# Two fused layers on one core: layer 1's experts computed on pairs sorted by expert

## The chip, the core and the metric

The program runs on one core of a Trainium2 chip. Five engines work side by side: TensorE (PE in the profile, its weight loads PEld), VectorE (DVE), ScalarE (ACT), GpSimd (POOL) and SyncE (SP), which issues most transfers. The metric is the device time in microseconds (us). The kernel before took 1327.2 us as the median of three runs (1326.11 to 1327.76).

## The reference

Four rows of 512 tokens with 128 channels pass through two layers. Both layers add an attention and a mixture of experts to the row, each computed from the same layer-normed input. Everything is float32.

- Layer 0, attention: for 16 heads and a band of 64 earlier positions, differences of projections pass through two 16 by 16 products with an exact GELU. The result is a logit for each of the 64 positions. A softmax over the band weighs the values.
- Layer 0, experts: 16 experts with a gated activation, the best four of a token weighted by a softmax.
- Layer 1, attention: 16 heads of 8 channels over all 512 positions of the row.
- Layer 1, experts, which the change is about:

```python
score = relu(xf @ rw1 + rb1) @ rw2 + rb2
_, topi = top_k(score, 2)
mask = zeros(bool).at[arange(T)[:, None], topi].set(True)
gate = softmax(where(mask, score, -inf))
for e in range(8):
    h = relu(xf @ W1[e] + b1[e])        # 128 -> 512
    y = h @ W2[e] + b2[e]               # 512 -> 128
    out = out + gate[:, e:e + 1] * y
```

The gate of an expert that a token did not choose is zero, so only two of the eight experts of a token reach its output.

## The kernel before

The state `x1` stays in SBUF: 16 tiles of 128 tokens by 128 channels, four to a row. Work is written as Python generators that yield at chosen points. `woven` takes a list of generators, each with the number of its yields, and always advances the one that is least far along. That sets the order in which instructions are written down. A planner then orders the instructions of each engine by that order, by priority (`tc.high_priority` moves some ahead) and by its own cost estimates; on each engine the final order is fixed.

**Layer 0** goes row by row. `band_logits(b)` (L555 to L637) runs 64 steps. Each subtracts shifted projections on DVE (L572, about 2000 elements a partition), applies the GELU on ACT (L574, L578), and reduces over channels on PE with four column tiles side by side (L586, high priority). `gated_experts(b)` (L659) holds the 16 experts of layer 0: products at L688, L695 and L675, DVE work at L671 to L673. `prepare(b+1)` projects the next row. Each row is woven in two parts: the first 24 steps of the logits (30 in row 0), then the other 37.

`band_values(b-1)` finishes the attention of the row before: skewed copies through DRAM (L314 to L344), products at L353 and L357. It stands in the first part of the next row.

`relu_experts(b)` is layer 1's mixture of experts. It normalises the row into `xn` and transposes it into `xT` (L408), which layer 1's attention also reads. It computes the router (L388 with `rw1`, L418), ranks the scores and makes a row of gates for each expert. Those rows go to DRAM and come back spread over all partitions (L444). For each of the 8 experts and each of four chunks of 128 hidden channels, `hidden` multiplies 128 weight columns by all 512 tokens of the row (L388) and applies the relu on ACT (L396). Four products for the expert before sum the second layer (L454). DVE multiplies by the gate row (L458) and POOL adds to `total` (L459). In float32 one matmul is recorded as two passes on PE. So a row has 8 x 8 matmuls of 512 columns, all experts for all tokens.

The experts of row b-1 are woven half into the second part of row b and half into the first part of row b+1. Row 2's second half and all of row 3's experts fall into layer 1.

**Layer 1's attention**, `full_attention`, is a list of steps. A step has two products of scores (L970, four row tiles side by side): one set is reduced to its maximum on DVE (L987), the other is exponentiated on ACT (L994). Every second step weighs values (L883). All of these have high priority. Explicit dependencies keep them in order; the next set of products waits for the reduction and the exponential that free its PSUM bank. `pace` holds the list of these products. Each `hidden` product is made to come after the product that was last in `pace` when it was written, which spreads the experts over the steps.

SP issues nearly all transfers in order: route rows, expert weights, the band's copies, stores of `out`. POOL issues only the zero fill at the start. `out` of a row is stored right after its attention is added (L918), for the last row at the very end (L1006).

Of the kernel before, what the change touches and what calls it, by code (L numbers as in the profile page):

```python
# [22 lines left out]
FP = mybir.dt.float32  # L23
AF = mybir.ActivationFunctionType
ALU = mybir.AluOpType
# [3 lines left out]
P = 128  # L29
# [10 lines left out]
F1 = 512  # L40
LIMIT = 7.0
# [5 lines left out]
    "ident": 128, "hmask": 8, "mask8": 8, "lt16": 256, "lt8": 64, "ones8": 1, "rep": 128,  # L47
}
# [10 lines left out]
def shape_constants():  # L59
# [13 lines left out]
        "rep": (p[:, None] == m[None, :] % BD),  # L73
    }
# [23 lines left out]
def two_layers(ctx: ExitStack, tc: tile.TileContext, w: dict, consts: bass.AP, out: bass.AP):  # L98
# [47 lines left out]
    rows = keep.tile([37, 128], FP, name="rows")  # L146
    nc.sync.dma_start(out=rows[0:32, :], in_=w["L1_ffn_b1"].rearrange("e (c f) -> (e c) f", f=128))
    nc.sync.dma_start(out=rows[32:36, :], in_=w["L1_ffn_rb1"].rearrange("(c f) -> c f", f=128))
    nc.sync.dma_start(out=rows[36:37, :], in_=w["L0_ffn_scale"][None, :])
# [18 lines left out]
    b2_1 = keep.tile([E1, C], FP, name="b2_1")  # L168
    nc.sync.dma_start(out=b2_1, in_=w["L1_ffn_b2"])
# [68 lines left out]
    def routes(pool, tag, g, n, k, less, dst):  # L238
# [15 lines left out]
        nc.vector.tensor_scalar(rank, rank, float(k), None, ALU.is_lt)  # L254
# [41 lines left out]
    route_d = [[dram.tile([n, T], FP, name=f"route{n}_{b}") for b in range(B)] for n in (E0, E1)]  # L296
# [88 lines left out]
    def hidden(wt, bias, b, c):  # L385

        ph = bank()
        mm = nc.tensor.matmul(ph, wt[:, c * P:(c + 1) * P], xT[:, b * T:(b + 1) * T], start=True, stop=True)  # L388
        if pace:
            tc.add_manual_dep(  # L390
                mm.ins, pace[-1].ins.name,
                mybir.DependencyInfo(mybir.DependencyClass.NoSync, mybir.DependencyReason.DATA),
                reason="experts spread over the steps",
            )
        h = chain.tile([P, T], FP, tag="h", name="h", bufs=5)
        nc.scalar.activation(h, ph, AF.Relu, bias=bias[:, c:c + 1])  # L396
        return h

    def relu_experts(b):


        xn = chain.tile([P, TPB, C], FP, tag="o", name="xn", bufs=1)
        rw1 = chain.tile([C, F1], FP, tag="ew1", name="rw1")
        nc.sync.dma_start(out=rw1, in_=w["L1_ffn_rw1"])
        layernorm(b, xn)
        yield
# [4 lines left out]
        for c in range(4):  # L411
            hs.append(hidden(rw1, cols[:, 32:36], b, c))
# [14 lines left out]
        route = small.tile([P, TPB, E1], FP, tag="route1", name="route1")  # L427
        routes(small, "pairs", scores, E1, K1, c_("lt8"), route)
        yield
        rT = route_rows(small, route, E1, route_d[1][b], 1.0)  # L430
        py = bank()
        nc.tensor.matmul(py, b2_1, rT, start=True, stop=True)
        total = chain.tile([C, T], FP, tag="total", name="total", bufs=1)
        nc.scalar.copy(total, py)
        yield
        old = None
        for e in range(E1 + 1):
            if e < E1:
                w1 = chain.tile([C, F1], FP, tag="ew1", name="ew1")
                nc.sync.dma_start(out=w1, in_=w["L1_ffn_W1"][e])  # L440
                w2 = chain.tile([P, 4, C], FP, tag="ew2", name="ew2")
                nc.sync.dma_start(out=w2, in_=w["L1_ffn_W2"][e].rearrange("(c p) d -> p c d", p=P))
                r = chain.tile([P, T], FP, tag="r", name="r")
                nc.sync.dma_start(out=r, in_=route_d[1][b][e].partition_broadcast(P))  # L444
            new = []
            if old:
                py = bank()
            for c in range(4):
                if e < E1:
                    new.append(hidden(w1, cols[:, e * 4:e * 4 + 4], b, c))  # L450
# [590 lines left out]
```

## Time and profile before

| | |
|---|---|
| median of three runs | 1327.2 us |
| the profiled execution's own time | 1327.88 us |
| its span, first to last instruction | 1326.1 us |
| mean granted TensorE clock | 0.933 |
| row 0 of layer 0 | 36 to 235.8 us |
| row 1 | 235.8 to 463.3 us |
| row 2 | 463.3 to 696.2 us |
| row 3 | 696.2 to 909.5 us |
| layer 1 | 909.5 to 1326.1 us |

A line of a group gives the source line, the engine, the operation, the tiles written and read, the shapes and how many there were. After the first bar come the busy time in us and the mean of one in ns. After the second comes the time for which the engine was idle just before, with what ended it. A line of the table of stretches gives the stretch, its length, and for each engine the busy time with the number of instructions in brackets; then the granted clock as a share of full speed, the share of the 16 DMA engines that was busy, and GB/s. A line of a timeline gives the start and the length in us, then the instruction, with the idle time before it and what ended it in square brackets. A line of the waits gives the sum in us, how often, and the longest.

### The profile page before, as it was taken

The page shows a single profiled execution, that of the slowest core. Times are in us where ns is not written, and L with a number is a line of the kernel's source. Part 1 is how long each engine was busy: PE and PEld are TensorE (multiplying, and loading weights), DVE is VectorE, ACT ScalarE, POOL GpSimd, SP SyncE. Part 2 cuts the span into 40 slices and gives each one's busy share as a digit, 9 for nine tenths or more (in the row PEclk, how much of TensorE's full clock was granted, in tenths as well). Part 3 has the DMA queues.
Part 4 walks back from the last instruction along what each step waited for, and adds up shares of the span by engine and source line. Part 5 has one row for each costly group of instructions (what it writes and reads, how often), then busy time and mean ns, then how long its engine had stood idle before and what let it go on. Part 6 is the DMA issues. An engine that isn't in the chain of part 4 may idle for free. (4 is left out here: it accounts for less than half of the span.)

```text
span 1326.1 us, 17391 instructions
## 1 busy us (share of the span) xinstructions
PE 1140.2 (86%) x6727; PEld 438.3 (33%) x6727; DVE 1011.4 (76%) x1085; ACT 1004.9 (76%) x1142; POOL 76.5 (6%) x72
## 2 busy tenths in 40 slices
PE   4677887577879968998997899897999899999997
PEld 2122233132434423343341234433333334333332
DVE  4999998999977899998789999873655556445451
ACT  4899997989988899999879999994255445545554
POOL 2000000000000100100000010003100000000000
PEclk9798888778979989998999999998899999999999
DMA  8121111264412345551234555124453130120100
GB/s 279 42 86 54 61 60 55 101 155 113 125 52 61 96 136 141 134 156 49 72 100 140 139 143 148 56 79 145 110 112 95 48 73 15 40 66 24 49 24 9
DMA packets 170348, 120.75 MB, mean 91 GB/s; under 512 B 66909, under 2 KB 149562, under 8 KB 168730
## 3 DMA queue, kind: packets, MB, share of 16 engines
q1 hardware_dynamic: 168794, 112.91, 31.1%
q0 software_dynamic: 1184, 6.29, 1.2%
q8 instruction: 54, 0.88, 0.3%
q10 hardware_dynamic: 288, 0.43, 0.1%
q14 instruction: 28, 0.23, 0.1%
HBM read 90.57 MB, written 29.03 MB: 90 GB/s over the span
## 5 line engine op out<-in xcount | busy, mean ns | idle before, releaser
L572 DVE TENSOR_TENSOR z<-proj 128x2044 f32<-128x2044 f32 (+31 forms) x256 | 556.3, 2194 | 23.1 <-PE lbank L586 14.3
L586 PE MATMUL lbank<-z,place 128*32 128x504 f32 (+18 forms) x2048 | 291.3, 646 | 98.8 <-ACT z L578 54.7
L987 DVE TENSOR_REDUCE nmax<-score 128x2 f32<-128x1024 f32 x128 | 156.3, 1225 | 174.0 <-PE score L970 166.3
L578 ACT ACTIVATE z<-z,posb 128x1024 f32<-128x1024 f32 (+31 forms) x256 | 266.5, 1097 | 9.3 <-DVE z L572 7.4
L574 ACT ACTIVATE z<-z,brep 128x2048 f32<-128x2048 f32 (+31 forms) x128 | 240.7, 1907 | 7.8 <-DVE z L572 7.5
L994 ACT ACTIVATE ex<-score 128x1024 f32<-128x1024 f32 x128 | 130.5, 1024 | 145.2 <-PE score L970 145.2
L388 PE MATMUL bank<-xT,ew 128*128 128x512 f32 x256 | 140.1, 636 | 3.8 <-DVE e L628 3.8
L586 PEld LDWEIGHTS lbank<-z,place 128*32 128x32 f32 x2048 | 44.3, 114 | 272.2 <-ACT z L578 133.3
L454 PE MATMUL bank<-h,ew 128*128 128x512 f32 x256 | 131.2, 611 | 2.1 <-ACT h L396 2.1
L396 ACT ACTIVATE h<-bank,cols 128x512 f32<-128x512 f32 x144 | 98.1, 684 | 37.8 <-PE bank L388 36.7
L459 POOL TENSOR_TENSOR total<-total,part 128x512 f32<-128x512 f32 x32 | 55.0, 1719 | 1020.1 <-DVE part L458 820.1
L970 PE MATMUL score<-kpad,qpad 32*128 32x512 f32 x384 | 109.9, 645 | 4.1 <-DVE nmax L987 3.2
L970 PE MATMUL score<-qa,kpad 32*128 32x512 f32 x384 | 103.5, 648 | 2.2 <-ACT ex L994 2.2
L675 PE MATMUL accbank<-wT,lin 128*128 128x128 f32 x512 | 81.3, 295 | 17.1 <-DVE lin L673 17.1
L675 PEld LDWEIGHTS accbank<-wT,lin 128*128 128x128 f32 x512 | 71.3, 203 | 64.4 <-issue 31.8
L688 PE MATMUL gbank<-tT,wT 128*128 128x512 f32 x128 | 72.6, 651 | 11.3 <-DMA wT<-wT_all 7.4
L883 PE MATMUL accbank<-ex,vaug 128*32 128x512 f32 x512 | 70.4, 616 | 0.2 <-ACT ex L994 0.2
L695 PE MATMUL gbank<-tT,wT 128*128 128x512 f32 x128 | 69.3, 624 | 0.0
L454 PEld LDWEIGHTS bank<-h,ew 128*128 128x128 f32 x256 | 43.3, 190 | 62.6 <-issue 51.9
L388 PEld LDWEIGHTS bank<-xT,ew 128*128 128x128 f32 x256 | 41.2, 194 | 64.0 <-issue 48.8
L691 ACT ACTIVATE glu<-gbank,gbt 128x512 f32<-128x512 f32 x64 | 43.8, 685 | 14.6 <-PE gbank L688 13.8
L671 DVE SCALAR_TENSOR_TENSOR lin<-lin,r 128x512 f32<-128x512 f32 x64 | 47.2, 737 | 6.4 <-ACT lin L697 4.9
(198 smaller groups left out, 1226.2 us busy)
## 6 DMA issues: line engine op xcount, KB each, us to landing
r<-route SPq DMA_DIRECT2D x96, 256.0 KB
ew<-in_L_ffn_W SPq DMA_DIRECT2D x64, 256.0 KB
wb<-by_s SPq DMA_DIRECT2D x32, 512.0 KB
wT<-wT_all SPq DMA_DIRECT2D x48, 192.0 KB
by_t<-e SPq DMA_DIRECT2D x8, 1024.0 KB
f<-by_t SPq DMA_DIRECT2D x128, 64.0 KB
by_s<-g SPq DMA_DIRECT2D x16, 512.0 KB
wb<-by_s SPq DMA_DIRECT2D x24, 256.0 KB
```

The lines of the kernel that those rows point to most:

```text
L388: mm = nc.tensor.matmul(ph, wt[:, c * P:(c + 1) * P], xT[:, b * T:(b + 1) * T], start=True, stop=True)
L396: nc.scalar.activation(h, ph, AF.Relu, bias=bias[:, c:c + 1])
L454: nc.tensor.matmul(py, old[1][:, c, :], old[0][c], start=(c == 0), stop=(c == 3))
L572: nc.vector.tensor_tensor(z[:, :, :, 0:n], seen, own, ALU.subtract)
L574: nc.scalar.activation(z[:, :, :, 0:n], z[:, :, :, 0:n], AF.Gelu, bias=b_dmg)
L578: last = nc.scalar.activation(z[:, dq, :, 0:n], z[:, dq, :, 0:n], AF.Gelu, bias=posb[:, j:j + 1])
L586: mm = nc.tensor.matmul(ps[q:q + 32, t0:T], place[:, kind, 3 - dd:35 - dd], z[:, dq, hg, 0:n], start=(dd == 0), stop=(dd == 3),)
L675: nc.tensor.matmul(ya[:, i * P:(i + 1) * P], lin[:, i * P:(i + 1) * P], wT[:, 2, :], start=False, stop=(e == E0 - 1 and i == TPB - 1),)
L688: nc.tensor.matmul(pg, wT[:, 0, :], tT, start=True, stop=True)
L970: mm = nc.tensor.matmul(ps[:, h - two, :], own[r, i * P:(i + 1) * P], seen[r, :], start=True, stop=True)
L987: freed.append(nc.vector.tensor_reduce(nmax[n % 2][:, i, two:two + 2, 8:9], ps, AX.X, ALU.max, negate=True))
L994: freed.append(nc.scalar.activation(ex[n, i][:, two:two + 2, :], ps, AF.Exp, scale=inv))
```

## The change

The experts of layer 1 are computed for two rows at a time, and only for the pairs of a token and an expert that it chose. Two rows have 1024 tokens and 2048 pairs. Sorted by expert, each expert's list padded to a multiple of 128, they fill at most 23 blocks of 128 pairs. All 23 are computed, whatever the routing.

- `begin(b)` is the first part of `relu_experts`: norm, transpose, router and ranks. It also stores `xn` to DRAM (`xs_d`). The gate rows in DRAM and their broadcast are gone.
- `pairs(s)` handles rows 2s and 2s+1. Two products with a triangle and with ones count the tokens ahead of each token for each expert. Some DVE operations turn these into each pair's place in the sorted list. Sixteen products with selections built on DVE (`sel`) turn the places into the list of tokens of each block (`whose`) and a list of weight rows of each block (`which`).
- For each block POOL issues an indirect transfer of the block's expert weights and biases (128 rows of 1156 numbers, `wx`) and one of its 128 token rows (`xb`). PE transposes the rows, makes four products of 128 columns for the hidden layer, and four for the second layer one block later. The relus are split between ACT and DVE, the second bias is added on DVE, and SP stores the block (`ys_d`).
- At the end 16 indirect transfers fetch each token's two results, and 16 DVE operations add them to `x1` with their gates.
- Rows 0 and 1 are done in layer 0: `begin(0)` in the second part of row 1, `begin(1)` and 14 steps of `pairs(0)` in the second part of row 2, 24 steps of it in the first part of row 3, the rest and `begin(2)` in the second part of row 3. Rows 2 and 3 are done in layer 1 beside the attention, after the band values of row 3 and `begin(3)`.
- `wx` has two buffers in layer 0 and three in layer 1. `dense` in the attention has one buffer instead of two. `out` of rows 2 and 3 is stored at the end.
- The program receives an array `pair_weights` made from the weights by copying alone, and some more constants.

```diff
+NS = 2 * TPB
+NB = (NS * P * K1 + E1 * (P - 1)) // P
+WX = 2 * F1 + 4 + C
...
+    def begin(b, pool, deep):
...
+        nc.sync.dma_start(
+            out=xs_d[b // 2][b % 2 * T:(b % 2 + 1) * T, :].rearrange("(t p) c -> p t c", p=P), in_=xn
+        )
...
+    def pairs(s, pool, deep):
...
+        nc.tensor.matmul(pt[:, 0:NS * E1], c_("upper"), flat, start=True, stop=True)
+        nc.tensor.matmul(pt[:, NS * E1:2 * NS * E1], ones, flat, start=True, stop=True)
...
+        for t in range(n2):
+            if not t % 4:
+                sel = pool.tile([P, 4, P], FP, tag="sel", name="sel", bufs=2)
+                nc.vector.tensor_tensor(
+                    sel, in_blk[:, 1, t:t + 4, None].to_broadcast([P, 4, P]),
+                    c_("along")[:, None, :].to_broadcast([P, 4, P]), ALU.is_equal,
+                )
+            nc.tensor.matmul(pt[:, 0:NB], sel[:, t % 4, :], tb[:, t, :], start=(t == 0), stop=(t == n2 - 1))
...
+        def fetch(to, rows, index):
+            nc.gpsimd.indirect_dma_start(
+                out=to, out_offset=None, in_=rows, in_offset=bass.IndirectOffsetOnAxis(ap=index, axis=0)
+            )
+
+        def weights(j):
+            wx[j] = pool.tile([P, WX], FP, tag="wx", name="wx", bufs=deep)
+            fetch(wx[j], w["pair_weights"], which[:, j:j + 1])
+
+        def load(g):
+            k = min(2, NB - 2 * g)
+            xb[g] = pool.tile([P, 2, C], FP, tag="xb", name="xb", bufs=2)
+            for i in range(k):
+                fetch(xb[g][:, i, :], xs[:, :], whose[:, 2 * g + i:2 * g + i + 1])
...
+        def second(j, h):
+            py = bank()
             for c in range(4):
...
+                nc.tensor.matmul(
+                    py[:, 0:C], h[:, c * P:(c + 1) * P], wx[j][:, F1 + c * P:F1 + (c + 1) * P],
+                    start=(c == 0), stop=(c == 3),
+                )
+            y = pool.tile([P, C], FP, tag="y", name="y")
+            nc.vector.tensor_tensor(y, py[:, 0:C], wx[j][:, 2 * F1 + 4:WX], ALU.add)
+            nc.sync.dma_start(out=ys[j * P:(j + 1) * P, :], in_=y)
...
+        for j in range(NB):
+            g = j // 2
+            if j + deep < NB:
+                weights(j + deep)
+            if j % 2 and 2 * (g + 1) < NB:
+                turn(g + 1)
+                if 2 * (g + 2) < NB:
+                    load(g + 2)
+            ph = bank()
+            for c in range(4):
+                mm = nc.tensor.matmul(
+                    ph[:, c * P:(c + 1) * P], wx[j][:, c * P:(c + 1) * P],
+                    xbT[g][:, j % 2 * P:(j % 2 + 1) * P], start=True, stop=True,
+                )
+                if not c:
+                    paced(mm)
+            h = chain.tile([P, T], FP, tag="h", name="h", bufs=4)
+            for c in range(4):
+                b1 = wx[j][:, 2 * F1 + c:2 * F1 + c + 1]
+                to = h[:, c * P:(c + 1) * P]
+                if c % 2:
+                    nc.vector.tensor_scalar(to, ph[:, c * P:(c + 1) * P], b1, 0.0, ALU.add, ALU.max)
+                else:
+                    nc.scalar.activation(to, ph[:, c * P:(c + 1) * P], AF.Relu, bias=b1)
+            yield
+            if late:
+                second(*late)
+            late = (j, h)
+            yield
...
+        for g in range(NS // 2 + 1):
+            if g < NS // 2:
+                got[g] = pool.tile([P, 2, 2, C], FP, tag="sel", name="got", bufs=2)
+                for i in range(2):
+                    for k in range(2):
+                        fetch(got[g][:, i, k, :], ys[:, :], place_[:, k, 2 * g + i:2 * g + i + 1])
+            if g:
+                for t in range(2 * g - 2, 2 * g):
+                    x = x1[:, s * NS + t, :]
+                    for k in range(2):
+                        nc.vector.scalar_tensor_tensor(
+                            x, got[g - 1][:, t % 2, k, :], gate[:, k, t:t + 1], x, ALU.mult, ALU.add
+                        )
+            yield
...
+        pq = l0.enter_context(tc.tile_pool(name="pairs0", bufs=1))
+        both = after(begin(1, pq, 2), pairs(0, pq, 2))
...
-                experts[b - 1] = relu_experts(b - 1)
-                second.append((experts[b - 1], 22))
-            if b > 1:
-                first.append((experts[b - 2], 22))
+            if b == 1:
+                second.append((begin(0, pq, 2), 6))
+            if b == 2:
+                second.append((both, 19))
+            if b == 3:
+                first.append((both, 24))
+                second.append((after(both, begin(2, pq, 2)), 27))
...
-            dense = work.tile([P, T], FP, tag="dense", name="dense")
+            dense = work.tile([P, T], FP, tag="dense", name="dense", bufs=1)
...
-            if b < B - 1:
+            if b < 2:
                 nc.sync.dma_start(out=x_out[:, b], in_=x1[:, b * TPB:(b + 1) * TPB, :])
...
+    pq = ctx1.enter_context(tc.tile_pool(name="pairs1", bufs=1))
     weave(
         (full_attention(), 106),
-        (after(woven((band_values(B - 1, ready[B - 1][1]), 23), (experts[B - 2], 42)), relu_experts(B - 1)), 22 + 42 + 79 + 4),
+        (after(band_values(B - 1, ready[B - 1][1]), begin(B - 1, pq, 3), pairs(1, pq, 3)), 22 + 5 + 58 + 2),
     )
-    nc.sync.dma_start(out=x_out[:, B - 1], in_=x1[:, (B - 1) * TPB:B * TPB, :])
+    for b in range(2, B):
+        nc.sync.dma_start(out=x_out[:, b], in_=x1[:, b * TPB:(b + 1) * TPB, :])
```

## The prediction

> **What bounds the kernel now.** I read the page's head first: no engine is full over the whole span, so the answer must come stage by stage.
>
> ```profile
> span 1326.1 us, 17391 instructions
> PE 1140.2 (86%) x6727; PEld 438.3 (33%) x6727; DVE 1011.4 (76%) x1085; ACT 1004.9 (76%) x1142; POOL 76.5 (6%) x72
> ```
>
> Next the busy times between the starts of the four rows of layer 0 (each begins where the two `e` subtractions of L628 of the row before end) and in layer 1 (the last line):
>
> ```profile
> core 0: us, PE busy (x) PEld busy (x) DVE busy (x) ACT busy (x) POOL busy (x), PEclk, DMA share, GB/s
> 36.00:235.80 199.80, 148.44 (x804) 56.20 (x796) 189.26 (x189) 179.85 (x211) 0.11 (x1) 0.85 0.20 61
> 235.80:463.30 227.50, 188.28 (x1155) 78.25 (x1156) 202.67 (x218) 203.19 (x220) 5.05 (x4) 0.89 0.37 100
> 463.30:696.20 232.90, 208.85 (x1224) 85.12 (x1223) 210.80 (x224) 211.18 (x236) 16.86 (x8) 0.96 0.41 113
> 696.20:909.50 213.30, 187.87 (x1155) 73.75 (x1153) 194.28 (x186) 194.43 (x212) 15.39 (x7) 0.98 0.41 113
> 909.50:1326.10 416.60, 387.78 (x2318) 135.31 (x2318) 197.96 (x238) 199.04 (x239) 30.57 (x25) 0.96 0.24 63
> ```
>
> Row 0 has no experts of layer 1 and runs DVE at 189.26/199.80 = 94.7%: that is a row's floor. Rows 1 to 3 stand at 89, 90.5 and 91% of DVE because PE, with experts woven in, is full in their second halves. In layer 1 PE is the bound (387.8 of 416.6). There I looked at when DVE's maxima start:
>
> ```profile
> 1207.67 1.23 DVE L987 TENSOR_REDUCE nmax<-score 128x2 f32<-128x1024 f32 x1
> 1210.21 1.23 DVE L987 TENSOR_REDUCE nmax<-score 128x2 f32<-128x1024 f32 x1 [1.31 <-PE score L970]
> ...
> 1222.24 1.23 DVE L987 TENSOR_REDUCE nmax<-score 128x2 f32<-128x1024 f32 x1 [1.90 <-PE score L970]
> ...
> 1224.78 1.23 DVE L987 TENSOR_REDUCE nmax<-score 128x2 f32<-128x1024 f32 x1 [0.82 <-PE score L970]
> ...
> 1227.91 1.23 DVE L987 TENSOR_REDUCE nmax<-score 128x2 f32<-128x1024 f32 x1 [1.91 <-PE score L970]
> ```
>
> An attention step is 2.54 us at its shortest (products 1.1, maximum 1.2, two handovers) and about 3.12 where PE has more to do. From 954 to 1292 us are 116 steps in 338 us, 2.91 each, PE 96.5% busy. So less PE work helps until 116 x 2.54 = 295 us, 43 us less, and no further.
>
> **The change, part by part.** The costs come from these groups and two timelines:
>
> ```profile
> L388 PE MATMUL bank<-xT,ew 128*128 128x512 f32 x256 | 140.1, 636 | 3.8 <-DVE e L628 3.8
> L454 PE MATMUL bank<-h,ew 128*128 128x512 f32 x256 | 131.2, 611 | 2.1 <-ACT h L396 2.1
> L396 ACT ACTIVATE h<-bank,cols 128x512 f32<-128x512 f32 x144 | 98.1, 684 | 37.8 <-PE bank L388 36.7
> L675 PE MATMUL accbank<-wT,lin 128*128 128x128 f32 x512 | 81.3, 295 | 17.1 <-DVE lin L673 17.1
> 479.28 3.25 POOL L459 TENSOR_TENSOR total<-total,part 128x512 f32<-128x512 f32 x1 [21.57 <-DVE part L458]
> 557.22 1.27 POOL L459 TENSOR_TENSOR total<-total,part 128x512 f32<-128x512 f32 x1 [10.33 <-DVE part L458]
> ```
>
> *Matmuls.* Removed: 512 records (two passes per matmul) of 512 columns at 271.3/512 = 0.53 us = 271 us. Added: 46 blocks x 8 matmuls x 2 passes = 736 records of 128 columns. The nearest row is L675, same widths: 81.3/512 = 0.159 us; 736 of them = 117 us. [...]
>
> *Layer 0, DVE.* 19 of the 32 `part` products and L459 adds (3, 8, 8 of them in rows 1 to 3) go: 19 x 0.685 = 13 us. L459 also holds up DVE: the L572 beside the add at 479.28 took 3.36 us, its group's median is 2.17; over the 18 adds of layer 0 such stretches sum to 15 us (2.9, 7.1, 5.1 by row). Added for the pair of rows 0 and 1: the sorting, some 45 small operations at 0.17 to 0.28 (as L259, L368) and about 10 of 368 to 512 elements at 0.53 to 0.69: 11.5 us, in row 2; per block two relus and one bias sum of 128 columns at 0.28 (L368): 0.84; 4 blocks in row 2, 19 in row 3; 16 final sums at 0.28 = 4.5 in row 3. One `add_rows` (0.68) goes in each of rows 2 and 3. DVE by row: 202.7 - 4.9 = 197.8; 210.8 - 13.3 + 14.9 = 212.4; 194.3 - 11.3 + 20.5 = 203.5. At row 0's 94.7% these take 208.9, 224.3 and 214.9 us: -18.6, -8.6, +1.6, together -26. PE no longer opposes: row 3 loses 65 us (its 128 L388 and L454 records without the router) and gains 19 x 2.7 = 51, so PE stands at 174 of 213; row 1 loses 30. ACT swaps 8 relus of 0.684 an expert for two of 0.3 (L655's 128 columns) and half a copy a block: less in rows 1 and 2, +-2 us in row 3.
>
> *Indirect transfers in layer 0.* 23 weight, 23 row and 16 result fetches = 62 on POOL. The trace has only direct transfers from POOL (0.53 us of POOL, L486, landing after 9.1 us in the opening burst) and none with an index. What one takes from DVE is bounded by 0 and by L459's mean stretch, 15.1/18 = 0.84 us: 0 to 52 us. [...] L459 reads 2 x 512 elements a partition, a fetch 1 index, so I take 0.2: +12 us.
>
> *Weights in time.* A block fetches 592 KB. Queue 1 moved 112.91 MB in 31.1% of 16 engines' span, 17.1 KB/us an engine, so 2.2 us with all 16 free and 4 to 7 at the 0.5 to 0.7 busy of these phases; with POOL's issue and landing 6 to 11 us. With two buffers the fetch for block j+2 waits for the second product and bias sum of block j; behind it in POOL's queue stands the next row fetch. Blocks come every 8 us in row 3 (12 while the first 24 steps of the logits run, some 100 us). A late weight stops PE in order and with it L586, whose slack is row 3's 213 - 174 us: 0 to 36 us (3 late x 12); four z buffers (8 us of DVE work) cover most: +4. With three buffers and 11 us a block layer 1 is safe.
>
> *Layer 1.* From 954 to 1292 stand 85 + 80 expert records, 0.48 us of PE's busy time each with overlaps counted once, 79 us, and 2 us of bias product and transposes: -81. Added, at the full clock of this stage: 368 records x 0.145 (its L819 and L913, 128 columns, take 0.14 to 0.18) = 53, 32 select passes x 0.12, 23 transposes x 0.15: +61. PE 326 - 20 = 306, at 96.5% 317 instead of 338: -21. That is 2.7 us a step, close to the floor, so I give 4 back for unevenness and for small DVE operations ahead of a maximum: -17. [...]
>
> *Ends and small parts.* At 1313.99 two last expert products stand for 2 us between the last weighing and its transposes: -2. Row 2's store moves before row 3's, +0.4 of SP issue. On SP, route and expert loads (which waited 147 and 102 us there for slots) give way to 46 stores that wait for the bias sum; behind them stand band values and gate weights, fewer waits than before. `dense` with one buffer makes the key copy wait for the query's store, but that was issued two steps (5 us) earlier: covered; uncovered 2 us on ACT x 3. The dropped `b1`, `b2` and route rows cost under 1 us.
>
> Sum against the profiled run's 1327.9 us: -26 + 12 + 4 - 17 - 2 = -29, 1299; the median lies 0.7 below it: **1298 us**.
>
> **Rivals.**
> - *Layer 1 at its floor*: products of 0.3 us fill the gaps of the steps, and fetches cost DVE nothing: 1327 - 26 - 43 - 2 = 1256. For it: pieces a quarter as long. Against: PE still needs 306 > 295.
> - *Fetches lock DVE* (slower): in rows 2 and 3 each of 62 fetches stretches DVE as L459 does or more. Without them the gain is 41; it decides from 41/62 = 0.66 us each. At 0.84: 1327 - 41 + 52 = 1338; at 1.1 (L459's full stretch) 1354.
> - *Late weights stop PE* (slower): 1294 without the 4 us above; 23 blocks of layer 0 each L us late cost 23 L less 39 of slack, even at L = 3.1; at 4, 1347. For it: two buffers, DMA at 0.5 to 0.7. Against: only row 3's first half has blocks this close. [...]
> - *Given back*: contention and lateness at half these prices, no measurable change, 1327.
>
> **How the numbers follow.** The forecast (1280 to 1318) 0.47, the floor 0.16, locked DVE 0.20, stopped PE 0.13, given back 0.04. Under 0.2% (2.7 us) this kernel's runs can't be told from no change. Faster: 0.47 + 0.16 = 0.63; same 0.04; slower 0.33. The range takes the floor case and most of both slow ones: 1256 to 1348.
>
> **What would show it.** Layer 1's steps near 2.7 us, PE near 310 in the stretch of 338; rows 1 to 3 of layer 0 near 210, 225 and 215 with DVE above 94%; narrow expert records near 0.15 us. Wrong: L572 medians in row 3 well over 2.17 (lock); PE or its weight loads waiting on `wx` or `xb` (late fetches); steps at 2.54 (floor).

## The result, and the profile after

The changed kernel takes 1408.05 us (median of four runs, 1403.72 to 1415.0) where the kernel before took 1326.65 us beside it: 1.063 times as long, 95% interval 1.057 to 1.068. The forecast was 1298 us with a range of 1256 to 1348; sign and range were both wrong. The profiled execution spans 1406.7 us against 1326.1, so 80.6 us have to be found.

The head of the changed kernel's page shows PE relieved and still a longer span: PE, DVE and ACT are each busy for a smaller share of it than before, so all three wait more.

```profile
span 1406.7 us, 18399 instructions
...
PE 1074.3 (76%) x7029; PEld 481.8 (34%) x7029; DVE 1038.2 (74%) x1301; ACT 955.6 (68%) x1119; POOL 174.1 (12%) x165
```

Busy times by row of layer 0 and in layer 1, cut as before at the ends of each row's two `e` subtractions (L628 before, L812 now):

```profile
core 0: us, PE busy (x) PEld busy (x) DVE busy (x) ACT busy (x) POOL busy (x), PEclk, DMA share, GB/s
36.00:235.90 199.90, 149.83 (x804) 55.37 (x804) 189.91 (x190) 180.72 (x214) 0.11 (x1) 0.85 0.20 61
235.90:449.60 213.70, 159.67 (x1084) 66.91 (x1084) 197.50 (x215) 189.33 (x200) 0.11 (x1) 0.87 0.35 93
449.60:677.10 227.50, 173.58 (x1174) 77.97 (x1174) 207.18 (x261) 196.47 (x213) 19.99 (x14) 0.86 0.37 100
677.10:971.70 294.60, 206.58 (x1365) 111.94 (x1365) 206.98 (x256) 188.94 (x226) 73.78 (x48) 0.82 0.41 114
971.70:1406.70 435.00, 365.65 (x2527) 160.28 (x2527) 220.47 (x346) 183.99 (x245) 71.35 (x73) 0.91 0.29 80
```

Rows 1 and 2 fell by 13.8 and 5.4 us. Row 3 went from 213.3 to 294.6: +81.3, with DVE's work (207 us) close to what was forecast (203.5) but its share at 70% instead of 95%. That is waiting, not work. The rest by position: the start of layer 1 (last `e` to first score product) 17.6 to 14.3, -3.3; first to last score of layer 1 383.8 to 388.8, +5.0; from the last score to the end 15.2 to 31.9, +16.7. Together -13.8 - 5.4 + 81.3 - 3.3 + 5.0 + 16.7 = +80.5.

What the engines wait for in row 3, from the list of waits of that stretch:

```profile
engine line waited for: us in total, times, longest us
ACT h L625 <- PE bank L612: 52.7, 14, 9.2
PE bank L612 <- DMA wx<-pair_weights,which: 47.0, 17, 5.3
DVE h L623 <- ACT h L625: 45.2, 15, 5.3
```

PE stands 17 times for late weights, and ACT and DVE stand behind PE, since the relus of the block lie in their order ahead of the band logits. The timeline of two blocks shows why the weights are late (start, duration, engine, line; in brackets the idle time before and what ended it):

```profile
871.27 0.29 DVE L591 TENSOR_TENSOR y<-bank,wx 128x128 f32<-128x128 f32 x1 [1.75 <-PE bank L586]
...
872.34 2.11 POOL L561 DMA_INDIRECT wx<-pair_weights,which  x1 [4.44 <-ACT h L625]
...
877.89 1.13 PE L612 MATMUL bank<-xbT,wx 128*128 128x128 f32 x8 [0.39 <-DMA wx<-pair_weights,which]
...
878.86 1.06 PE L586 MATMUL bank<-wx,h 128*128 128x128 f32 x8
...
879.95 0.29 DVE L591 TENSOR_TENSOR y<-bank,wx 128x128 f32<-128x128 f32 x1
881.02 2.64 POOL L561 DMA_INDIRECT wx<-pair_weights,which  x1 [6.57 <-ACT z L762]
...
887.35 2.04 PE L612 MATMUL bank<-xbT,wx 128*128 128x128 f32 x8 [3.15 <-DMA wx<-pair_weights,which]
```

Read it as a ring. The bias sum `y` of block j-1 (871.27) frees its weight buffer; the fetch for block j+1 starts 1.07 us later; hidden(j+1), the first product, starts when its weights are there, at 877.89 at the earliest; only behind that on PE stands second(j), the second product of the block before (878.86), whose `y` (879.95) frees the next buffer. With two buffers, each fetch waits for a product that itself stands behind a wait for the fetch before. Nothing is prefetched: one block takes 8.7 us in the first ring (871.27 to 879.95) and 13.0 in the next (to 892.93). From the third block's `y` to the last one's (679.8 to 943.4) are 20 blocks, 13.2 us each.

The ring holds nearly throughout. Of the 20 weight fetches from the fourth block on, 19 begin within 0.8 us after the `y` that frees their buffer, and 19 first products begin within 0.2 us after their weights have landed. One turn of it takes 13.8 us on average over these 20: 1.0 us from `y` to the fetch, 6.5 from the fetch to the first product, 4.1 from there to the second product of the block before (1.0 in the first ring above, up to 10.2 where PE's order has other products in between), and 2.2 to the end of its `y`.

In layer 1 the maxima come at the floor of 2.54 us more often than before (81 of 127 steps against 56), but around the router and the sorting of rows 2 and 3 they come late. Such starts of L1175 at the sorting:

```profile
1117.59 1.23 DVE L1175 TENSOR_REDUCE nmax<-score 128x2 f32<-128x1024 f32 x1 [1.74 <-PE score L1158]
...
1121.54 1.23 DVE L1175 TENSOR_REDUCE nmax<-score 128x2 f32<-128x1024 f32 x1 [2.72 <-PE score L1158]
...
1125.85 1.22 DVE L1175 TENSOR_REDUCE nmax<-score 128x2 f32<-128x1024 f32 x1
...
1130.48 1.23 DVE L1175 TENSOR_REDUCE nmax<-score 128x2 f32<-128x1024 f32 x1 [0.48 <-PE score L1158]
...
1135.39 1.22 DVE L1175 TENSOR_REDUCE nmax<-score 128x2 f32<-128x1024 f32 x1
```

The steps here are 4.0 to 4.9 us, the next one 8.1. The third and fifth maximum have no idle time before them: small DVE instructions of gates and sorting ran up to their start. The 24 maxima from 1066.7 to 1153.2 take 86.5 us; the same 24 of the kernel before took 72.0. All other maxima took 280.2 us against 289.8. So the lighter experts gave 9.6 us and the sorting's stage took 14.5.

The tail:

```profile
1378.42 0.29 DVE L591 TENSOR_TENSOR y<-bank,wx 128x128 f32<-128x128 f32 x1 [14.09 <-PE bank L586]
...
1381.29 0.94 POOL L561 DMA_INDIRECT got<-ys,place__7240  x1 [32.87 <-issue]
...
1382.54 0.95 POOL L561 DMA_INDIRECT got<-ys,place__7240  x1 [0.30 <-issue]
...
1400.02 0.95 POOL L561 DMA_INDIRECT got<-ys,place__7240  x1 [0.30 <-issue]
...
1402.99 0.35 DVE L644 SCALAR_TENSOR_TENSOR x<-got,gate,x 128x128 f32<-128x128 f32 x1 [1.33 <-DMA got<-ys,place__7240]
```

The last block's result is ready at 1378.7, and 16 fetches follow at 1.25 us each (0.95 and a gap of 0.30), 20 us on POOL alone, with one sum on DVE behind each.

### The profile page after: what moved, and what is told of

It is laid out like the page before. It is cut to its first block, busy times and chain, and to the rows that moved or that the text cites. A ratio compares the mean times of both kernels' runs of the same rounds, so it can differ in the third digit from the quotient of the medians.

```text
span 1406.7 us, 18399 instructions
## 1 busy us (share of the span) xinstructions
PE 1074.3 (76%) x7029; PEld 481.8 (34%) x7029; DVE 1038.2 (74%) x1301; ACT 955.6 (68%) x1119; POOL 174.1 (12%) x165
## 5 line engine op out<-in xcount | busy, mean ns | idle before, releaser
L756 DVE TENSOR_TENSOR z<-proj 128x2044 f32<-128x2044 f32 (+31 forms) x256 | 548.4, 2164 | 8.4 <-ACT proj L702 6.0
L770 PE MATMUL lbank<-z,place 128*32 128x504 f32 (+18 forms) x2048 | 312.8, 691 | 124.0 <-ACT z L762 69.9
L762 ACT ACTIVATE z<-z,posb 128x1024 f32<-128x1024 f32 (+31 forms) x256 | 265.9, 1097 | 15.7 <-DVE z L756 13.7
L1175 DVE TENSOR_REDUCE nmax<-score 128x2 f32<-128x1024 f32 x128 | 156.3, 1225 | 149.2 <-PE score L1158 149.1
L758 ACT ACTIVATE z<-z,brep 128x2048 f32<-128x2048 f32 (+31 forms) x128 | 240.8, 1906 | 13.8 <-DVE z L756 12.7
L561 POOL DMA_INDIRECT wx<-pair_weights,which x46 | 59.5, 1294 | 645.6 <-DVE lin L855 196.8
L612 PE MATMUL bank<-xbT,wx 128*128 128x128 f32 x368 | 70.5, 331 | 49.4 <-DMA wx<-pair_weights,which 48.0
L859 PEld LDWEIGHTS accbank<-wT,lin 128*128 128x128 f32 x512 | 71.4, 208 | 71.0 <-DVE lin L857 45.8
L625 ACT ACTIVATE h<-bank,wx 128x128 f32<-128x128 f32 x92 | 33.5, 365 | 82.9 <-PE bank L612 68.2
L612 PEld LDWEIGHTS bank<-xbT,wx 128*128 128x128 f32 x368 | 56.8, 226 | 94.1 <-issue 65.7
L872 PE MATMUL gbank<-tT,wT 128*128 128x512 f32 x128 | 73.5, 658 | 13.6 <-DMA wT<-wT_all 10.5
L623 DVE TENSOR_SCALAR h<-bank,wx 128x128 f32<-128x128 f32 x92 | 32.0, 348 | 62.9 <-ACT h L625 61.8
L561 POOL DMA_INDIRECT xb<-xs,whose x46 | 62.3, 1354 | 90.8 <-PE bank L579 45.4
L586 PE MATMUL bank<-wx,h 128*128 128x128 f32 x368 | 63.2, 306 | 4.1 <-DVE e L812 3.2
L586 PEld LDWEIGHTS bank<-wx,h 128*128 128x128 f32 x368 | 52.1, 209 | 39.4 <-issue 30.1
```

What stands on the lines that cost most here:

```text
L561: nc.gpsimd.indirect_dma_start(out=to, out_offset=None, in_=rows, in_offset=bass.IndirectOffsetOnAxis(ap=index, axis=0))
L586: nc.tensor.matmul(py[:, 0:C], h[:, c * P:(c + 1) * P], wx[j][:, F1 + c * P:F1 + (c + 1) * P], start=(c == 0), stop=(c == 3),)
L612: mm = nc.tensor.matmul(ph[:, c * P:(c + 1) * P], wx[j][:, c * P:(c + 1) * P], xbT[g][:, j % 2 * P:(j % 2 + 1) * P], start=True, stop=True,)
L756: nc.vector.tensor_tensor(z[:, :, :, 0:n], seen, own, ALU.subtract)
L758: nc.scalar.activation(z[:, :, :, 0:n], z[:, :, :, 0:n], AF.Gelu, bias=b_dmg)
L762: last = nc.scalar.activation(z[:, dq, :, 0:n], z[:, dq, :, 0:n], AF.Gelu, bias=posb[:, j:j + 1])
```

## The experiments

The theory was that the ring of fetch, first product and second product makes row 3 long, and the 16 fetches the tail. Rivals: the relus that go to and fro between ACT and DVE, the fetches themselves, and the order of DVE's instructions. Where a row or a stage is given, it comes from the profile of that run. Row 3 is a noisy yardstick: in the runs that left the ring alone it took 283 to 297 us.

**Second product first.**

```
             ph = bank()                  # block j
+            if late: second(*late)       # block j-1, now ahead of hidden(j)
+            yield
             for c in range(4): ... matmul(ph ...)   # hidden(j)
             ... relus ...
-            yield
-            if late: second(*late)
             late = (j, h)
```

> The second product of the block before is written ahead of the block's hidden product; nothing else is changed. Theory A (late weights: with two buffers and the second product standing behind the next hidden product on PE, a block's buffer comes free only after the next block has started, so fetches run one after another, about 12.7 us a block in row 3): row 3 of layer 0, 294.6 us, falls by 30 to 70, the whole from about 1407 to 1340 to 1375. Theory B (the relus hand over between ACT and DVE four times a block): row 3 stays above 280.

Measured: 1361.26 us, ratio to the kernel before 1.031 (1.022 to 1.039). Row 3 took 247.4 us, 47.2 less, and with it nearly the whole gain: at its start the two kernels are 2.7 us apart, and layer 1 and the tail are as they were (391.3 and 31.5). A block takes 10.5 us instead of 13.2. The window of row 3 and the line of its waits that answers to the 47.0 above:

```profile
674.40:921.80 247.40, 190.93 (x1359) 101.56 (x1357) 206.94 (x255) 189.62 (x227) 71.91 (x47) 0.90 0.48 135
```

```profile
PE bank L615 <- DMA wx<-pair_weights,which: 3.9, 3, 2.3
```

PE waits three times for weights, 3.9 us in all, instead of 17 times and 47.0. The work and the bytes are the same, written in another order (with which the planner's order on DVE and ACT shifts too): the order was the cause. The granted clock rose too, from 0.82 to 0.90 in this row, and PE's busy time fell from 206.6 to 190.9 us for the same products (more on this at the end).

**All relus on ACT.**

```
-                if c % 2: nc.vector.tensor_scalar(to, ph[...], b1, 0.0, ALU.add, ALU.max)
-                else:     nc.scalar.activation(to, ph[...], AF.Relu, bias=b1)
+                nc.scalar.activation(to, ph[...], AF.Relu, bias=b1)
```

> All four relus of a block on ACT instead of two on ACT and two on DVE. Theory B (DVE waited 45 us in row 3 for ACT's relus and ACT for DVE's): row 3 falls by 30 or more, to 265 or less. Theory A (late weights): row 3 changes by less than 20 us, since the relus follow the late product.

Measured: 1395.46 us (two runs, 1388.4 and 1402.52), row 3 297.3. The waits of L623 for L625 are gone and the row is no shorter; PE waits 54.8 us for weights in 15 blocks. The handing to and fro was a symptom and falls as a cause. The few us less lie in rows 1 and 2 and within what runs differ by.

**Weights only once.**

```
         def weights(j):
+            if deep == 2 and j >= 2:
+                wx[j] = wx[j - 2]
+                return
```

> In layer 0 only the first two blocks' weights are fetched and all 23 blocks use them in turn, so no block waits for weights; the output of rows 0 and 1 therefore leaves out the other experts. Theory A: row 3 falls from 294.6 to 215 to 235 us, the whole to 1330 to 1350. Theory B: row 3 stays above 270.

Measured: 1360.16 us, ratio 1.030 (1.021 to 1.039), row 3 238.0 us, 56.6 less; from the third to the last `y` a block takes 9.0 us.

```profile
675.40:913.30 237.90, 186.75 (x1365) 101.60 (x1365) 206.04 (x255) 186.81 (x223) 38.95 (x29) 0.87 0.35 94
```

Taking the transfers away gives little more than writing the second product first. Against the 294.6 us of the profile above, two independent edits put 47 to 57 of row 3's 81 us on the ring (35 to 59 if the whole spread of 283 to 297 is allowed for); the medians of the whole kernel fell by 47 and 48. They also agree that 23 to 33 us over the forecast's 215 have another cause.

**Without the last fetches.** The 16 final fetches and sums of rows 2 and 3 are left out.

```
-        for g in range(NS // 2 + 1):
+        for g in range(NS // 2 + 1 if s == 0 else 0):
```

> The last 16 fetches and sums of rows 2 and 3 are left out, and with them these rows' experts in the output. If the end (31.9 us from the last scores to the end, 15.2 before) is lengthened by 16 fetches of 1.25 us in a row on POOL: -16 to -20 us, whole 1387 to 1391. If it is lengthened by the last block's second product on PE (until 1378), less than 6 us.

Measured: 1383.9 us. The tail is 12.7 us instead of 31.9: 19.2 us, what 16 fetches at 1.25 us make. Row 3, which the edit doesn't touch, was 284.3 in this run; the rest of the difference is within what runs differ by, row 3's spread above all.

**Sums of rows 0 and 1 in layer 1.** The last loop of `pairs(0)` becomes a track of its own in layer 1.

```
         (full_attention(), 106),
+        (collect(0, pq), 40),
```

> The 16 final fetches and sums of rows 0 and 1 are moved out of the end of layer 0's row 3 into the first fifth of layer 1, on a track of their own; nothing else changes. Theory: in the changed kernel the last 28 us of row 3, after the last block's bias sum, hold 16 fetches in a row at 1.25 us each on POOL (20 us), and DVE's sums, which wait for them in order, stand ahead of the row's two last e subtractions. Away from there row 3 falls by about 20 us (294 to about 275), and layer 1, where POOL and DVE have idle time, grows by at most 3: 1390 us (1380 to 1398). Rival: the late weights alone set row 3, and the router of row 2 and its gates hold the e subtractions anyway: row 3 stays within 5 us and the time is 1403 to 1412.

Measured: 1410.64 us, no gain. The fetches and sums were only written later, and were still put into the gap between the layers: on POOL the last of the 16 starts at 974.1 and the fills of `wqk`, `qpad` and `kpad` that layer 1 needs begin at 975.0, behind it. The lag from the last `e` to the first maximum grew from 16.5 to 25.0, and row 3 was 284.4, within its spread. The order of the program isn't the order of the engines: here work that was ready was drawn forward.

**Layer 1's experts end early.**

```
-        (after(band_values(...), begin(...), pairs(1, pq, 3)), 22 + 5 + 58 + 2),
+        (after(band_values(...), begin(...), pairs(1, pq, 3)), 22 + 5 + 58 + 22),
```

> One number of the order of layer 1 is changed: the track with the experts of rows 2 and 3 counts 107 places instead of 87, so that its last block and its fetches and sums are written into the attention at four fifths of it instead of behind it. Theory: the 16 fetches at 1.25 us are what the tail consists of (31.9 us after the last scores against 15.2 before); under the attention they cost nothing, and the attention's steps at the end run at their floor instead: tail about 14 us, scores from first to last longer by 0 to 5 us, total 1393 us (1387 to 1400). Rival: the blocks pressed into fewer steps lengthen those by as much as the tail gives, since PE is full there: 1403 to 1412.

Measured: 1439.77 us, 32 slower than the changed kernel: worse than either theory. The tail fell to 12.4 us, but first to last score rose from 388.8 to 444.7. The longest step, 16.7 us at 1169.4, lies far ahead of the last fetches: blocks now follow each other so closely that weights come late in layer 1 too (PE waits 4.9 us for them there and 3.0 at another place, none in the changed kernel), with score products behind them in PE's order.

**Three moves, and the same with the sorting spread.** Second product first, rows 0 and 1's sums in layer 1, early end; then eight more pauses in layer 1's sorting (`if s: yield` between its instructions), with the track at 115 places.

> Three moves at once, nothing left out: block j-1's second product is written ahead of block j's first on PE; the final sums of rows 0 and 1 are taken in layer 1; layer 1's experts end at four fifths of its attention. If the three losses are separate, the time is 1361 (with the first move alone) - 20 - 17 = 1324 us, row 3 about 227 us and the tail about 14. If row 3 is bound by DVE's order and not by the fetches, and layer 1 by PE, the sum isn't reached: row 3 stays at 240 or more, layer 1 gains nothing, 1345 to 1361.

> As the run with three moves, but layer 1's sorting (some 45 small DVE instructions and 16 select products) is written with eight more pauses between them, and the track counts 115 places, so that fewer of them stand ahead of one maximum. Theory: the five steps of 4 to 8 us around the sorting (36 us for eight maxima against 21 at the floor) come from DVE and PE work standing in order ahead of scores and maxima; spread, they lose half of the 15 us: 8 us below the run with three moves, about 1316. Rival: the same work is only moved to other steps that are no slacker, or those steps wait for the rows' output products: within 3 us of the run with three moves.

Measured: 1381.03 us (1.045, 1.039 to 1.050) and 1374.18 us (1.038, 1.032 to 1.045), both slower than the first move alone. Row 3 is 246.7 and 244.0, the tails 12.7 and 11.8, but the scores take 428 and 429 us. DVE's instructions between two maxima near the end of the run with three moves:

```profile
1300.55 1.23 DVE L1181 TENSOR_REDUCE nmax<-score 128x2 f32<-128x1024 f32 x1 [1.12 <-PE score L1164]
...
1304.45 0.38 DVE L650 SCALAR_TENSOR_TENSOR x<-got,gate,x 128x128 f32<-128x128 f32 x1 [2.08 <-DMA got<-ys,place]
1305.78 0.35 DVE L650 SCALAR_TENSOR_TENSOR x<-got,gate,x 128x128 f32<-128x128 f32 x1 [0.94 <-DMA got<-ys,place]
1307.04 0.35 DVE L650 SCALAR_TENSOR_TENSOR x<-got,gate,x 128x128 f32<-128x128 f32 x1 [0.91 <-DMA got<-ys,place]
...
1313.28 0.35 DVE L650 SCALAR_TENSOR_TENSOR x<-got,gate,x 128x128 f32<-128x128 f32 x1 [0.94 <-DMA got<-ys,place]
1313.55 1.22 DVE L1181 TENSOR_REDUCE nmax<-score 128x2 f32<-128x1024 f32 x1
```

Eight sums of 0.35 us stand ahead of the second maximum; each waits for its own fetch, and fetches come every 1.25 us. The step is 13.0 us, the next 10.2. The early end took the fetches' 20 us out of the tail and put more into the steps: first to last score grew by 39.5 us, of which these two steps hold 18. A second part lies earlier in the layer, in a step of 10.3 us:

```profile
1000.72 1.23 DVE L1181 TENSOR_REDUCE nmax<-score 128x2 f32<-128x1024 f32 x1 [1.91 <-PE score L1164]
...
1005.56 0.66 PE L362 MATMUL bank<-wb,va 128*32 128x128 f32 x8 [4.88 <-DMA wb<-by_s]
...
1011.01 1.23 DVE L1181 TENSOR_REDUCE nmax<-score 128x2 f32<-128x1024 f32 x1 [9.06 <-PE score L1164]
```

The track of the experts begins with the band values of row 3. Counting more places writes them earlier as well, and PE waits in order for their copies (`wb`). The spread sorting did what it was meant to at its place: the three groups of eight maxima around it take 32.8, 22.6 and 20.8 us against 32.7, 26.0 and 26.1 without, 8.6 us less. The total is 6.9 less, with intervals that overlap, so that the gain as a whole isn't shown.

**Sums apart from their fetches, and all together.** All 16 fetches first, into free weight buffers; the sums later, those of rows 0 and 1 tied to score products, those of rows 2 and 3 behind the last step (track at 95 places). The second run adds the second product first and the spread sorting, with the track at 105.

```
+        for g in range(NS // 2): ... paced(fetch(got[g][:, i, k, :], ys[:, :], place_...))
+    def add_up(s): ... paced(nc.vector.scalar_tensor_tensor(x, got[g][:, t % 2, k, :], gate..., x, ...))
+        (collect(0, pq), 60),
+    for _ in add_up(1): pass            # behind the attention
```

> Nothing is left out. The final fetches of both pairs go first, all 16 in a row into two weight buffers that are free by then, and the 16 sums come later: for rows 0 and 1 both are tied to layer 1's score products (in its first third), for rows 2 and 3 the sums stand behind the last step. The run that moved rows 0 and 1's sums without such a tie gave nothing: the sums and POOL's fetches were put ahead of layer 1's first maxima and of POOL's fills of wqk, so row 3 fell by 10 us and the start of layer 1 came 8.5 us later; the run that ended early lost its tail's 23 us to maxima that stood behind waiting sums. Theory: waiting sums in DVE's order are the cost, not the fetches. Tied, row 3 is about 284, the lag to the first maximum 16.5 or less, the tail 22 or less: 1408 - 10 - 12 = 1386 us (1378 to 1394). Rival: the fetches themselves set those times, or the sums cost wherever they stand: 1400 or more.

> Nothing is left out. Three moves together: block j-1's second product ahead of block j's first (-47 us alone), sums apart from their fetches as in the run before, layer 1's sorting with eight more pauses (it took about 9 us from the maxima around the sorting when it was tried); the track of layer 1's experts counts 105 places for 95 pauses. Theory: the three losses lie in different stages and add up: 1361 - 22 - 9 = 1330 us (1318 to 1342), row 3 near 238, the tail near 20. Rival: what is taken from one stage returns in layer 1, as with the early end (scores from first to last 391 to 430): 1350 or more.

Measured: 1415.48 us (1.069, 1.062 to 1.076) and 1375.21 us (1.041, 1.033 to 1.048). Both miss, to the side of the rivals. Of their parts one came out as hoped and one not. With the ring open, taking the fetches and sums out of row 3 does help: 234.3 us in the second run against 247.4 with the first move alone. (In the run with three moves they were only written later and still ran from 905.7 us on, inside row 3, which took 246.7. With the ring closed no gain shows: 289.1 in the first run, within the spread.)

```profile
674.10:908.40 234.30, 187.03 (x1359) 99.97 (x1357) 202.27 (x240) 190.80 (x229) 54.94 (x31) 0.93 0.49 137
```

But first to last score takes 421.8 and 432.1 us, 33 to 43 more than in the changed kernel, although no sum waits in DVE's order now. Part of it is spread over the stage; the longest single step is 10.7 us, beside the last 16 fetches. There a maximum begins 5.3 us after the modelled end of its scores, and the profile names no instruction that released it ("remote"); ACT's exponential begins only at 1383.91, after a wait of the same kind:

```profile
1377.50 1.06 PE L1178 MATMUL score<-qa,kpad 32*128 32x512 f32 x2
...
1383.85 1.23 DVE L1195 TENSOR_REDUCE nmax<-score 128x2 f32<-128x1024 f32 x1 [9.44 <-remote]
```

**Neither weights nor sums late.** The weights-once edit and the sums apart together.

> Layer 0 fetches the weights of the first two blocks only and uses these two in turn for all 23 blocks of rows 0 and 1 (the other experts are left out there), with the sums apart from their fetches as two runs above. It asks what row 3 is when neither weights nor sums are late. If these two are the whole of row 3's excess, it comes to the forecast's own 215 us (210 to 222) and the time to about 1330. If the relus, the row fetches or the order of PE's work hold it too, it stays at 228 to 240, 1340 to 1350.

Measured: 1357.74 us, row 3 228.7 us: at the lower edge of the rival's numbers.

```profile
674.20:902.90 228.70, 185.49 (x1365) 99.86 (x1365) 200.88 (x239) 190.49 (x226) 22.94 (x13) 0.89 0.35 92
```

Late weights and sums explain 66 of row 3's 81 us; about 14 over the forecast's 215 stay with the rest. DVE's work is 200.9 us here, 2.6 less than the forecast's 203.5, which held 4.5 us of sums that now lie elsewhere; its share is 88% instead of 94.7%. So the missing 14 us are waits of DVE, for which no single cause was isolated.

**Sixteen fetches more.** The changed kernel with 16 idle fetches in a row in layer 1's first third; the order on PE, DVE and ACT is untouched.

```
+        (burst(pq), 60),
```

> The changed kernel with 16 fetches more: the rows that the last fetches of rows 0 and 1 brought are fetched once again, in a row, in layer 1's first third, into weight buffers that are free there, and nothing reads them; the order of the instructions on PE, DVE and ACT stays what it was. It asks whether a series of fetches costs anything by itself. In the runs with an early end and with the sums apart, steps of 5 to 13 us stood beside such series even where no sum waited in DVE's order: in one of them a maximum began 5.3 us after the end of its scores. If a series by itself delays the engines, the steps beside it take 10 to 20 us more in all and the time is 1416 to 1428 us. If only the order of the instructions around it did (products of blocks and transposes ahead of scores), the steps stay at 2.54 and the time within 4 us of the changed kernel's 1408.

Measured: 1404.44 us, ratio 1.065 (1.059 to 1.071), like the changed kernel. Two maxima and fetches beside them:

```profile
1000.81 0.94 POOL L658 DMA_INDIRECT idle<-ys,place  x1 [0.30 <-issue]
...
1003.58 1.23 DVE L1190 TENSOR_REDUCE nmax<-score 128x2 f32<-128x1024 f32 x1 [0.74 <-PE score L1173]
1006.11 1.23 DVE L1190 TENSOR_REDUCE nmax<-score 128x2 f32<-128x1024 f32 x1 [1.31 <-PE score L1173]
```

First to last score took 389.7 us (388.8 without them), and the first 16 steps, beside which the fetches run, 38.9 us, against 35.4 to 39.3 in nine runs that have none there. The series of fetches cost the engines nothing that shows by itself, in this third of the layer; such a series cost whoever waited for it in order (a step of 13.0 us in the run with three moves). In the run with the sums apart the same steps took 45.8 us, so there it was not the fetches' presence. The traces name one part of what layer 1 lost: in all six runs in which the experts' track counts more places (95 to 115 for 87), PE waits 7 to 11 us there for the copies of row 3's band values, against 0.7 to 2.9 in the runs that leave the count alone. Those edits changed the order of instructions in many places of layer 1 at once; what the rest of the loss is made of stays open, as does the wait of 5.3 us.

None of these versions is as fast as the kernel before. The best without anything left out is the first move alone, 1361 us.

## Why the prediction was wrong, point by point

Forecast (-29 us) and profile (+80.6) are 110 us apart: 72 of them in layer 0's rows, 22 in layer 1's scores and 19 at the end, with 3 gained back at the start of layer 1.

- *Weights in time* is the step that failed. It took +4 out of a range of 0 to 36 us; the ring cost 47 (order changed) to 57 us (transfers removed). The text had the right dependency, that the fetch for block j+2 waits for the second product and bias sum of block j, and nearly the right landing time: the fetches took from 4.3 to 9.4 us to land, half of them under 5.9, where 6 to 11 were forecast. It then compared a landing of 6 to 11 us with blocks every 8 us, as if fetches ran ahead. What it left out is PE's queue: second(j) stands behind hidden(j+1), which waits for the fetch before. A fetch is thus begun only after its predecessor has been used; the prefetch depth is one, whatever the two buffers suggest. It also said that four z buffers cover a stall. Relus lie in ACT's and DVE's order between the z operations, so both engines stopped with PE (52.7 and 45.2 us). That layer 1 with three buffers would be safe was right: PE waited for no weights there.
- The rival *Late weights stop PE* had the effect, late weights that stop PE, though not PE's order as its reason. At L = 4, which it priced, its formula gives 23 x 4 - 39 = 53 us, about what the ring cost; its 1347 lacks the losses of layer 1 and of the end. 0.13 was too little.
- *Layer 0, DVE*: rows 1 and 2 were forecast at 208.9 and 224.3 and took 213.7 and 227.5. That is right within 5 us, with DVE at 92% and 91% of them and not 94.7%. Row 3's 214.9 holds for the work, not for the waits; besides the ring, 16 fetches and sums at its end cost about 9 to 13 us (247.4 to 234.3 and 238.0 to 228.7 where they were moved away). The step counted those sums as 4.5 us of DVE work and not as a wait for 16 fetches of 1.25 us. The remaining 14 us of row 3 have no cause that was isolated.
- *Indirect transfers in layer 0* put 12 us on DVE, 0.2 us a fetch, which was the author's estimate; no run shows it. The z products' medians by row are 2.15 to 2.17 us, their longest 2.29 against 3.36 before: DVE lost nothing. The rival *Fetches lock DVE* is out. But the two do meet: it was POOL's fetch that took longer, up to 2.93 us instead of 0.94 (last section). That lengthens the ring: over the 20 weight fetches from the fourth block on, the time on POOL beyond 0.94 us sums to 15.7 us, an estimate of what it can have added to row 3.
- *Matmuls*: 133.7 us busy in L612 and L586 for 736 records, 0.182 each, where 0.159 was taken (117 us). Against the 0.53 us of the wide records that is 0.34. In layer 1, 348 records took 0.168 against the forecast's 0.145.
- *Layer 1*: -17 forecast, +5 measured. Steps did go to the floor of 2.54 in places, and the stage without the sorting gave 9.6 us. The sorting and gates, costed as DVE time only for row 2 of layer 0, took 14.5 us in layer 1, where small instructions in DVE's and PE's order stood ahead of maxima and scores; spreading them took 8.6 us off three groups of eight maxima there. Seven steps of 5.3 to 5.6 us remain over the layer; in two of them (at 1206.8 and 1344.3) PE runs 12 and 16 passes of a block's two products, and a weighing, ahead of the next scores. Whether that is their cause was not tested.
- *Ends and small parts*: -2 forecast, +16.7 measured. The step saw two wide products leave the tail and missed that 16 fetches of 1.25 us, which can't start before the last block, enter it; without them it is 12.7 us.

## What to carry to other kernels

A prefetch was here only as deep as the order of the engine that frees its buffer: a block took 13.2 us with the second product behind the next block's first, and 10.5 with it ahead. Follow the release through that engine's queue: where the releasing instruction stands behind the user of the next fetch, as here, two buffers act as one. Many small indirect fetches were cheap while something else ran (16 more in layer 1: 389.7 us from first to last score against 388.8) and dear where consumers waited for them one by one, at the end of a stage (19.2 us of the tail) or in an engine's order ahead of critical work (a step of 13.0 us). Moving such work in the program mostly moved its cost elsewhere; each move should be read by stage, since here a gain in the tail (19.5 us with the early end) came back as a larger loss in the steps (55.9).

## What the runs showed of the hardware that was not expected

An indirect fetch of 128 rows took 0.94 us of POOL with a gap of 0.30 us to the next, whether it brought 64 KB or 592 KB. In layer 1 all 62 took 0.93 to 0.97, with medians of 942 ns for weights and 945 ns for token rows. In layer 0 the median was 1.07, the mean 1.51 and the longest 2.93 us, while the z products on DVE ran at their usual length (2.15 beside a fetch, 2.13 without one): where the two met, the fetch took longer and the z product did not. The trace shows which instruction held which fetch:

```profile
871.55 2.08 DVE L756 TENSOR_TENSOR z<-proj 128x1844 f32<-128x1844 f32 x1
872.34 2.11 POOL L561 DMA_INDIRECT wx<-pair_weights,which  x1 [4.44 <-ACT h L625]
...
880.76 2.08 DVE L756 TENSOR_TENSOR z<-proj 128x1848 f32<-128x1848 f32 x1
881.02 2.64 POOL L561 DMA_INDIRECT wx<-pair_weights,which  x1 [6.57 <-ACT z L762]
```

Both fetches begin inside a z product and end 0.82 us after it ends (873.63 and 874.45; 882.84 and 883.66). In layer 0, 29 of the 62 fetches took more than 1.2 us. Each of them began while DVE ran an instruction with two inputs in SBUF (25 times a z product) and ended 0.81 to 0.84 us after that instruction. One fetch is an exception: at 734.99 it began inside a z product and took 0.94. In layer 1, 13 fetches began beside a maximum, which reads PSUM, and took no longer than the others (0.93 to 0.95). In the other direction nothing was held: the 21 z products that began during a fetch took 2.02 to 2.27 us, 2.14 in the median. What in those instructions holds a fetch was not shown, since no run changed where their inputs lie.

PE's products were slower in row 3 where PE was kept waiting. With the ring closed they took 206.6 us of busy time at a granted clock of 0.82 (the changed kernel), 200.3 at 0.84 (all relus on ACT) and 199.3 at 0.85 (without the last fetches); with it open (order changed or transfers taken away) 190.9 at 0.90 (second product first), 186.8 at 0.87 (weights only once), 187.0 at 0.93 (all together) and 185.5 at 0.89 (neither late). PE waited 43.5 to 54.8 us for weights in the first three and 3.9 with the second product first. In these runs waits on PE thus went together with slower products; what ties the two was not tested. How much of row 3's time that makes was not measured apart, since PE's busy time isn't what bounds the row.
